# Products as pairs of 64 weight columns, and seven block products for eight in the aggregations of stage three

## Chip, cores and metric

The kernel runs on one core of a Trainium2 chip. The metric is the device time of one launch in microseconds; lower is better. All data are float32. "Graph" below means one of the 32 items of the batch.

## What is computed

A stack of four graph layers over 32 graphs of 512 nodes with 128 features each. Each layer starts with a layer norm and a Relu, and its result is added to its input. The third layer ("stage three") is itself four feature layers with skip connections; it is where most of the change lies.

```python
def _layer(nodes, adj, ws, bs, wd, bd, wn, bn, wu, bu):      # stage three
    src = nodes @ ws + bs
    src_agg = jnp.einsum('bjv,bij->biv', src, _l2norm(adj, 2))
    dst = nodes @ wd + bd
    dst_agg = jnp.einsum('bjv,bji->biv', dst, _l2norm(adj, 1))
    self_rep = nodes @ wn + bn
    upd = jnp.concatenate([src_agg, self_rep, dst_agg], axis=2)
    return jnp.tanh(upd @ wu + bu)
...
    h = jnp.maximum(_layernorm(x, axis=-1), 0.0)
    x = x + _L0_gnn_ref(h, adj, ...)      # one aggregation with the normed adjacency, leaky relu
    h = jnp.maximum(_layernorm(x, axis=-1), 0.0)
    x = x + _L1_gnn_ref(h, adj, ...)      # two aggregations, elu before, tanh after
    h = jnp.maximum(_layernorm(x, axis=-1), 0.0)
    x = x + _L2_gnn_ref(h, adj, ...)      # stage three: four of the layers above
    h = jnp.maximum(_layernorm(x, axis=-1), 0.0)
    x = x + _L3_gnn_ref(h, adj, ...)      # message, aggregation, GRU gates
```

## The kernel before, in words

**Plan.** The kernel first records every operation (`Plan.op`, line 135) with its engine, an assumed duration (`t_mm`, `t_tt` and the like, lines 319 to 335), and the buffers that it reads and writes. `Plan.order` (line 173) then runs a list schedule over all 32 graphs: each engine takes the operation with the earliest due time, `batch * PERIOD` less the length of the work that hangs on it, whose inputs are there and for whose buffers a place is free. The places are a fixed number per kind (line 299): 8 banks of PSUM, and SBUF tiles of 2, 4 and 8 KB per partition (`s2` 36, `s4` 5, `s8` 10). The order that results is the order of the instructions on each engine; work of two to three graphs is interleaved. Where the plan sees TensorE idle for over 0.7 us, `kept_warm` puts in products of the identity (`ps_idle`, line 1170).

**Data.** An adjacency `a` and its transpose `aT` are 128 partitions by 4 chunks by 512 columns, 8 KB each, loaded anew for each graph on SP's queue. Node features lie either in rows (128 nodes of a chunk on the partitions) or turned (features on the partitions, 512 nodes in the columns). Turning is done by a VectorE transpose of 32x32 blocks and a bounce through DRAM (`turned`, line 705), or, in the first two and the last graph, on TensorE against the identity.

**Products.** `mm` (line 352) records one TensorE product: 128 weight columns, and 128 to 512 columns of data, into one PSUM bank. An aggregation is four such products of 512 columns, one per chunk of 128 nodes. Products of 256 and 128 columns are recorded by `product` in `gates` (515), `seven` (833) and `fifteen` (913).

**Stage three.** After the first two layers, `a` and `aT` are scaled in place, column by column, with the roots of the squared sums (line 1096). The loop at line 1107 then goes through the four feature layers:
- layer 0: `paired_rows` (779) projects the features to source and destination rows `sd`; a node product and eight aggregation products of 512 columns add up in one bank; ScalarE's tanh reads that bank (1136).
- layer 1: `fifteen` (869) turns the features, aggregates them with `aT` and `a` (eight products of 512 columns, `ps_agg<-aT,f1r` and `ps_agg<-a,f1r`, copied out by ScalarE at 894), and then makes layer 1's result and its shares in layers 2 and 3 with fifteen products of 256 columns.
- layer 2: as layer 0, and VectorE adds the share from `fifteen` (1135) before the tanh.
- layer 3: the projections of two feature blocks are made by `seven` (796), a scheme of seven products for eight on halves of nodes and of inputs, with some fourteen VectorE operations; then aggregation as in layer 2.

**GpSimd** takes the power -1/2 for the norms (688) and for the scaling (1077), little else. In the norms, a VectorE operation (`nb`, 696) waits for it.

Of the kernel before, what the change touches and what calls it, by code (L numbers as in the profile page):

```python
# [24 lines left out]
PERIOD = 37.0  # L25
ENDING = -3.5
# [5 lines left out]
GATES = 5 * D  # L32
FIFTEEN = GATES + 4 * D
T_COLS = FIFTEEN + 6 * D
# [247 lines left out]
def gnn_stack(  # L282
# [16 lines left out]
    plan = Plan(sb, psum, {"bank": 8, "s2": 36, "s4": 5, "s8": 10}, {"bank": 0, "s2": 4, "s4": 0, "s8": 0})  # L299
# [12 lines left out]
    def wt(col, n=D):  # L312
        return w_sb[:, col:col + n]
# [37 lines left out]

    def mm(ps, out_of, lhs, rhs, n, start, stop, reads, later=0.0):
        op("PE", t_mm(n), lambda: nc.tensor.matmul(out_of(ps.ap()), lhs(), rhs(), start=start, stop=stop),  # L353
           reads, [ps], later=later)

    LAST = [W_L2[3][0] + (2 * k + o) * D for k in (2, 0) for o in range(2)]
# [11 lines left out]
    def setup():  # L368
# [67 lines left out]
        for at, (b11, b12, b21, b22), wbuf in ((0, LAST, (W2F, {3})), (GATES, BOTH, W3)):  # L436
# [11 lines left out]
        m, c = rf_sb, ROW_OF[3] * 2 * D  # L448
        op("DVE", t_tt(D), lambda: nc.vector.tensor_sub(t_sb[:, 4 * D:5 * D], m[:, c:c + D], m[:, c + D:c + 2 * D]), [RF], [(TS, {4})])
# [33 lines left out]
    def program(b):  # L483
# [13 lines left out]
        def gates(h3T, mT):  # L497
# [17 lines left out]
            def product(o, data, weight, wbuf, first):  # L515
                op("PE", t_mm(H), lambda: nc.tensor.matmul(o[0](), weight(), data[0](), start=first, stop=True, skip_group_check=True), [data[1], wbuf], [o[1]])  # L516

# [209 lines left out]
        def added_rows(x, m, quiet=False):  # L727

            o = buf("s2", rows_shape, "xr")
            if at_ends:  # L730
                ps = plan.bank("t")
                for c in range(NC):
                    op("PE", 0.109, lambda c=c: nc.tensor.transpose(ps.ap()[:, c * P:(c + 1) * P], m.ap()[:, c * P:(c + 1) * P], ident),
                       [m, ID], [(ps, {c})])
# [14 lines left out]
        def transposed(h, name):  # L749
            if at_ends:  # L750
                ps, hT = plan.bank("t"), buf("s2", name=name)
                for c in range(NC):
                    op("PE", 0.109, lambda c=c: nc.tensor.transpose(ps.ap()[:, c * P:(c + 1) * P], h.ap()[:, c, :], ident),
                       [(h, {c}), ID], [(ps, {c})])
                op("ACT", t_act(N), lambda: nc.scalar.copy(hT.ap(), ps.ap()), [ps], [hT])
                return hT
# [22 lines left out]
        def paired_rows(nodes, wcols, wbuf, bias, bbuf, col):  # L779

            sd = buf("s4", (P, NC, 2 * D), "sd")
            for h in range(NC // 2):
                ps = plan.bank("sd")
                for j in range(2):
                    c = 2 * h + j
                    for k, nk in enumerate(nodes):
                        mm(ps, lambda t, j=j: t[:, j * 2 * D:(j + 1) * 2 * D],
                           lambda nk=nk, c=c: nk.ap()[:, c * P:(c + 1) * P],
                           lambda k=k: wt(wcols + k * 2 * D, 2 * D), 2 * D, k == 0, k == len(nodes) - 1, [nk, wbuf])
# [6 lines left out]
        def seven(x1, x2, dst, part, behind):  # L796
# [3 lines left out]
            at = 0  # L800
            (b11, b12, b21, b22), wbuf, (bias, bc), bbuf = LAST, (W2F, {3}), (rf_sb, ROW_OF[3] * 2 * D), RF
            H = N // 2
            s13, s24, ev, dv, xx = (buf("s2", (P, 2, H), k) for k in ("s13", "s24", "ev", "dv", "xx"))
            bank_a, bank_b, bank_c, bank_d = (plan.bank("seven") for _ in range(4))

            def half(m, k):
                return m.ap()[:, k * H:(k + 1) * H]

            def t(k):
                return t_sb[:, at + k * D:at + (k + 1) * D]  # L810

            def dve(o, a, b, reads, writes, sub=False, behind=()):
                op("DVE", t_tt(H), lambda: nc.vector.tensor_tensor(o(), a(), b(), op=ALU.subtract if sub else ALU.add), reads, writes, behind=behind)

            def place(k, o):
                return lambda: dst(k, o)

            def of(m, k):
                return lambda: m.ap()[:, k, :]

            def flat2(m, k):
                return lambda: m.ap()[:, k, :].rearrange("p (j v) -> p j v", j=2)

            def region(ps, k):
                return lambda: ps.ap()[:, k * H:(k + 1) * H]

            def region2(ps, k):
                return lambda: ps.ap()[:, k * H:(k + 1) * H].rearrange("p (j v) -> p j v", j=2)

            def along2(m, c):  # L830
                return lambda: m[:, None, c:c + D].to_broadcast([P, 2, D])

            def product(ps, k, lhs, rhs, reads, behind=()):
                for j in range(2):
                    op("PE", t_mm(D), lambda j=j: nc.tensor.matmul(  # L835
                        ps.ap()[:, k * H + j * D:k * H + (j + 1) * D], lhs()[:, j * P:(j + 1) * P], rhs(),
                        start=True, stop=True), reads, [ps], behind=behind)

            def pair(m):
                return lambda: m.ap().rearrange("p k (j v) -> p k j v", j=2)  # L840


            dve(of(s13, 1), lambda: half(x1, 0), lambda: half(x1, 1), [x1], [(s13, {1})], True, behind)
            product(bank_a, 0, lambda: half(x1, 0), lambda: wt(b11), [x1, wbuf], behind)
            product(bank_a, 1, of(s13, 1), lambda: t(2), [(s13, {1}), (TS, {at + 2})])
            dve(flat2(ev, 0), region2(bank_a, 0), along2(bias, bc + D), [bank_a, bbuf], [(ev, {0})])
# [22 lines left out]
        def fifteen(f1, shares):  # L869
# [70 lines left out]
            def result(i, o):  # L940
                return half(out_of[o], i)
# [279 lines left out]
```

## Time and profile before

| | |
|---|---|
| time, median of 3 runs | 2272.33 us (2272.28 to 2272.53) |
| the profiled execution | 2275.95 us, of it the span from first to last instruction 2274.2 us |
| TensorE clock granted | 1.000 of full speed |
| idle products | 126 MATMUL records, 17.8 us |
| DMA | 263.03 MB, mean 116 GB/s |

The table of costly groups is read so: line, engine, operation, output and inputs by name, size of the weights, size of the data, count; then busy time in all and the mean duration of one; then the idle time of the engine ahead of them. For TensorE, durations of neighbouring products overlap, so the mean of 593 ns is not what a product costs. Some rows that the change touches:

```profile
L353 PE MATMUL ps_agg<-a,sd 128*128 128x512 f32 x768 | 385.3, 593 | 0.0
L353 PE MATMUL ps_agg<-aT,sd 128*128 128x512 f32 x768 | 380.5, 593 | 0.4 <-DVE sd L791 0.2
L353 PE MATMUL ps_sd<-w_sb,f 128*128 128x256 f32 x512 | 145.6, 380 | 0.9 <-ACT f L1112 0.9
L353 PE MATMUL ps_agg<-aT,f1r 128*128 128x512 f32 x256 | 130.7, 592 | 0.0
L1135 DVE TENSOR_TENSOR c<-ps_agg,c 128x512 f32<-128x512 f32 x64 | 43.7, 683 | 4.1 <-PE ps_agg L353 4.0
L813 DVE TENSOR_TENSOR s<-f,s 128x256 f32<-128x256 f32 x64 | 27.0, 422 | 13.1 <-ACT f L1136 13.1
```

### The profile page before, as it was taken

Reading aid. Unit: us, or ns where it says so; the run is one execution under the profiler, and the core shown is the slowest. Engines: PE = TensorE matmul, PEld = TensorE weight load, DVE = VectorE, ACT = ScalarE, POOL = GpSimd, SP = SyncE. Lnnn points to the kernel's source line nnn. Section 1 sums busy time; section 2 is a strip of 40 time slices with the busy share of each in tenths; the row PEclk is TensorE's granted clock in tenths of the full one; section 3 lists DMA queues with packets and bytes.
Section 4 is the critical chain, followed back from the end, with each engine's and each line's share of the span. In section 5 each row is a group of like instructions: output and inputs, shape, how many; then the busy total and the mean of one; then the engine's idle time right before and its main releaser. Section 6 shows DMA issues by size and latency. Waiting matters only on the chain.

```text
span 2274.2 us, 25755 instructions
## 1 busy us (share of the span) xinstructions
PE 2263.3 (100%) x7608; PEld 1311.8 (58%) x7608; DVE 1607.0 (71%) x4346; ACT 1101.4 (48%) x2563; POOL 216.6 (10%) x203
## 2 busy tenths in 40 slices
PE   9999999999999999999999999999999999999999
PEld 6555565555565555555555655555555556555556
DVE  6756676767777777767777777777677777776655
ACT  7643554544445544455544455445555444552422
POOL 2100100100100100001001001000010010010000
PEclk9999999999999999999999999999999999999999
DMA  8032333444333443334443334443344333333212
GB/s 295 29 105 77 111 99 117 139 128 127 119 105 121 130 130 120 107 117 135 132 123 121 104 120 130 130 120 108 115 136 134 122 117 106 121 99 91 79 42 65
DMA packets 199052, 263.03 MB, mean 116 GB/s; under 512 B 25984, under 2 KB 130688, under 8 KB 198912
## 3 DMA queue, kind: packets, MB, share of 16 engines
q1 hardware_dynamic: 198624, 261.26, 37.6%
q8 instruction: 60, 0.98, 0.2%
q14 instruction: 80, 0.66, 0.1%
q10 hardware_dynamic: 288, 0.13, 0.0%
HBM read 199.18 MB, written 62.13 MB: 115 GB/s over the span
## 4 chain that ended last, share of the span: by engine, by line
PE 95%; DMA 2%; DVE 2%; ACT 0%; issue 0%; SPq 0%; POOL 0%; ACTq 0%; DVEq 0%; POOLq 0%
PE ps_agg L353 61%; PE ps_fifteen L914 9%; PE ps_sd L353 7%; PE ps_seven L835 4%; PE ps_seven L516 4%; PE ps_upd L353 3%; PE ps_gate L353 3%; PE ps_lin L353 1%; PE ps_msg L353 1%; PE ps_node L353 1%; DMA last<-turn_last 0%; DMA turned<-turn_turned 0%; DMA bounce<-invT 0%; DMA r_sb<-in_brow 0%; DMA turn_turned<-blk 0%; DMA rows<-bounce 0%
## 5 line engine op out<-in xcount | busy, mean ns | idle before, releaser
L353 PE MATMUL ps_agg<-a,sd 128*128 128x512 f32 x768 | 385.3, 593 | 0.0
L353 PE MATMUL ps_agg<-aT,sd 128*128 128x512 f32 x768 | 380.5, 593 | 0.4 <-DVE sd L791 0.2
L688 POOL TENSOR_TENSOR sc<-v,neg_half 128x4 f32<-128x4 f32 (+1 forms) x127 | 150.6, 1186 | 1710.5 <-DVE v L649 1603.5
L353 PEld LDWEIGHTS ps_agg<-aT,sd 128*128 128x128 f32 x768 | 136.6, 191 | 86.4 <-issue 77.5
L700 ACT ACTIVATE h<-xr,nb,sc 128x128 f32<-128x128 f32 x384 | 157.9, 482 | 49.1 <-DVE nb L696 49.1
L353 PEld LDWEIGHTS ps_agg<-a,sd 128*128 128x128 f32 x768 | 137.0, 191 | 62.0 <-issue 53.8
L353 PE MATMUL ps_sd<-w_sb,f 128*128 128x256 f32 x512 | 145.6, 380 | 0.9 <-ACT f L1112 0.9
L353 PEld LDWEIGHTS ps_sd<-w_sb,f 128*128 128x128 f32 x512 | 94.4, 190 | 77.6 <-issue 61.7
L1136 ACT ACTIVATE f<-c,cf_sb 128x512 f32<-128x512 f32 x64 | 46.2, 722 | 179.8 <-DVE c L1135 179.8
L353 PE MATMUL ps_agg<-f,w_sb 128*128 128x512 f32 x256 | 130.9, 593 | 0.1
L353 PE MATMUL ps_agg<-aT,f1r 128*128 128x512 f32 x256 | 130.7, 592 | 0.0
L353 PE MATMUL ps_agg<-a,f1r 128*128 128x512 f32 x256 | 130.7, 592 | 0.0
L353 PE MATMUL ps_agg<-aT,h 128*128 128x512 f32 (+2 forms) x260 | 128.7, 583 | 0.6 <-ACT h L673 0.6
L353 PE MATMUL ps_agg<-a,rep 128*128 128x512 f32 x256 | 125.5, 592 | 0.0
L353 PE MATMUL ps_agg<-aT,rep 128*128 128x512 f32 x256 | 121.6, 595 | 2.0 <-DVE rep L1049 1.8
L353 PE MATMUL ps_agg<-aT,msg 128*128 128x512 f32 (+1 forms) x264 | 116.7, 579 | 0.0
L791 DVE TENSOR_TENSOR sd<-ps_sd,rf_sb 128x512 f32<-128x512 f32 x128 | 87.9, 687 | 32.3 <-PE ps_sd L353 31.9
L1096 DVE TENSOR_TENSOR a<-a,rows 128x512 f32<-128x512 f32 x128 | 87.2, 687 | 16.7 <-PE ps_agg L353 16.1
L709 DVE STREAM_TRANSPOSE blk<-h 128x512 f32<-128x512 f32 x87 | 61.4, 706 | 51.4 <-ACT h L700 51.2
L1077 POOL TENSOR_TENSOR inv<-stat,neg_half 128x8 f32<-128x8 f32 x32 | 59.4, 1857 | 308.8 <-DVE stat L1076 287.9
L1096 DVE TENSOR_TENSOR aT<-aT,rows 128x512 f32<-128x512 f32 x128 | 86.4, 684 | 2.0 <-PE ps_agg L353 1.9
L1136 ACT ACTIVATE f<-ps_agg,cf_sb 128x512 f32<-128x512 f32 x32 | 22.0, 687 | 131.8 <-PE ps_agg L353 131.8
(229 smaller groups left out, 4424.6 us busy)
## 6 DMA issues: line engine op xcount, KB each, us to landing
aT<-in_adjt SPq DMA_DIRECT2D x124, 512.0 KB, 3.9
turn_turned<-blk SPq DMA_DIRECT2D x696, 64.0 KB, 1.8
turned<-turn_turned SPq DMA_DIRECT2D x174, 256.0 KB, 2.7
a<-in_adj SPq DMA_DIRECT2D x62, 512.0 KB, 7.5
rows<-bounce SPq DMA_DIRECT2D x32, 512.0 KB, 3.7
shares<-bounce SPq DMA_DIRECT2D x32, 512.0 KB, 4.4
x<-in_x SPq DMA_DIRECT2D x32, 256.0 KB, 2.7
out<-xr SPq DMA_DIRECT2D x31, 256.0 KB, 3.1
```

The lines of the kernel that those rows point to most:

```text
L353: op("PE", t_mm(n), lambda: nc.tensor.matmul(out_of(ps.ap()), lhs(), rhs(), start=start, stop=stop), reads, [ps], later=later)
L516: op("PE", t_mm(H), lambda: nc.tensor.matmul(o[0](), weight(), data[0](), start=first, stop=True, skip_group_check=True), [data[1], wbuf], ...
L688: op("POOL", t_pow(n), lambda: nc.gpsimd.tensor_tensor(inv.ap()[:, :n], v8.ap()[:, :n], neg_half[:, :n], op=ALU.pow), [v8, NH], [(inv, {0})])
L700: op("ACT", t_act(D, 2), lambda c=c: nc.scalar.activation(h.ap()[:, c, :], xin.ap()[:, c, :], AF.Relu, bias=nb.ap()[:, c:c + 1], scale=inv ...
L709: op("DVE", t_tt(N), lambda: nc.vector.transpose(blk.ap().rearrange("p b (c r) -> p c b r", c=NC), m.ap().rearrange("p c (b s) -> p c b s" ...
L791: op("DVE", t_tt(N), lambda ps=ps, h=h: nc.vector.tensor_add(sd.ap()[:, 2 * h:2 * h + 2, :], ps.ap().rearrange("p (j v) -> p j v", j=2), a ...
L835: op("PE", t_mm(D), lambda j=j: nc.tensor.matmul(ps.ap()[:, k * H + j * D:k * H + (j + 1) * D], lhs()[:, j * P:(j + 1) * P], rhs(), start= ...
L914: op("PE", t_mm(H), lambda: nc.tensor.matmul(o[0](), weight(), data[0](), start=first, stop=True, skip_group_check=True), [data[1], wbuf], ...
L1077: roots = op("POOL", t_pow(2 * NC) + 0.4, lambda: nc.gpsimd.tensor_tensor(inv.ap()[:, :2 * NC], stat.ap(), neg_half, op=ALU.pow), [stat, N ...
L1096: op("DVE", t_tt(N), lambda m=m, c=c, s=s: nc.vector.tensor_mul(m.ap()[:, c, :], m.ap()[:, c, :], rows.ap()[:, s, :]), [(m, {c}), rows], [ ...
L1136: end = op("ACT", t_act(N, 1), lambda to=to, i=i, f_new=f_new: nc.scalar.activation(f_new.ap(), to.ap(), AF.Tanh, bias=cf_sb[:, i:i + 1]), ...
```

## The change

**Every product in two halves.** `by_halves` issues a product as two, with weight columns 0 to 63 into PSUM partitions 0 to 63 and weight columns 64 to 127 into partitions 64 to 127, over the same data. All of `mm`, the gates' and `fifteen`'s products, the turns on TensorE and the idle products go through it. Each half is issued as a 128x64 tile of the array, at column 0 or 64.

**Seven products for eight in stage three.** The aggregations of the four feature layers are taken as products of 2x2 blocks: two halves of the 128 features, two chunks of nodes, two halves of the 512 columns. The blocks of `a` and `aT` get three combinations each, `made_of`, four GpSimd subtractions of 512 columns per matrix (one in place). The features get four combinations, `left_sums`, on VectorE. `side_by_side` issues two unlike 64-column products as a pair, one on each half of the array; `features` (layers 0, 2 and 3) and `edges` (layer 1) list them and add their results, mostly with VectorE operations of 64 partitions by 256 columns, some on GpSimd. `nodes` products join the same banks by three 256-column products. `seven` is gone: layer 3's projections are plain products of `paired_rows` over two feature blocks.

**Plan.** `PERIOD` 37 to 41, `ENDING` -3.5 to -5.5; places `s2` 26, `s4` 6, a new kind `s6` 5 for the combinations, `s8` 8.

```diff
-PERIOD = 37.0
-ENDING = -3.5
+PERIOD = 41.0
+ENDING = -5.5
...
+HALVES = slice(0, P // 2), slice(P // 2, P)
...
-    plan = Plan(sb, psum, {"bank": 8, "s2": 36, "s4": 5, "s8": 10}, {"bank": 0, "s2": 4, "s4": 0, "s8": 0})
+    plan = Plan(sb, psum, {"bank": 8, "s2": 26, "s4": 6, "s6": 5, "s8": 8}, {"bank": 0, "s2": 3, "s4": 0, "s6": 0, "s8": 0})
...
+    def by_halves(to, weight, data, start, stop):
+        for c in HALVES:
+            nc.tensor.matmul(to[c], weight[:, c], data, start=start, stop=stop, skip_group_check=True)
+
     def mm(ps, out_of, lhs, rhs, n, start, stop, reads, later=0.0):
-        op("PE", t_mm(n), lambda: nc.tensor.matmul(out_of(ps.ap()), lhs(), rhs(), start=start, stop=stop),
-           reads, [ps], later=later)
+        op("PE", t_mm(n), lambda: by_halves(out_of(ps.ap()), lhs(), rhs(), start, stop), reads, [ps], later=later)
...
+        H, Q = N // 2, D // 2
...
+        def made_of(m):
+            tm, even, odd = buf("s6", (P, 2, 3, H), "made"), {0, 2}, {1, 3}
...
+            for o, x, y, reads, writes in (
+                    (t(1), two(m, 1, 1), two(m, 0, 1), [m], [(tm, {1})]),
+                    (two(m, 0, 1), two(m, 0, 1), two(m, 0, 0), [(m, even)], [(m, even)]),
+                    (t(0), two(m, 1, 1), two(m, 0, 1), [m], [(tm, {0})]),
+                    (t(2), two(m, 1, 0), t(0), [(m, odd), (tm, {0})], [(tm, {2})])):
+                summed("POOL", nc.gpsimd, t_pool(N), o, x, y, -1, reads, writes)
+            return tm
...
+        def left_sums(n, part, src, st, place):
+            for k, x, y, sign, reads in (
+                    (0, part(1, 0), part(1, 1), 1, []), (1, place(0), part(0, 0), -1, [0]),
+                    (2, part(0, 0), part(1, 0), -1, []), (3, part(0, 1), place(1), -1, [1])):
+                summed("DVE", nc.vector, t_tt(n), place(k), x, y, sign, [src] + [(st, {j}) for j in reads], [(st, {k})])
+
+        def side_by_side(lo, hi, begun):
+            for pair in zip(lo, hi, strict=True):
...
+                def emit(emits=emits):
+                    for to, lhs, rhs, start in emits:
+                        nc.tensor.matmul(to(), lhs(), rhs(), start=start, stop=True, skip_group_check=True)
+
+                op("PE", t_mm(H), emit, reads, writes)
+
+        def features(i, sd, nodes, made, f_new, more):
...
+            lo = products(A, 1, q4) + products(C, 5, q4) + node(C, 1, 1) + products(A, 2, q4) + node(A, 0, 0) + products(C, 3, q2)
+            hi = products(Bh, 6, q4) + node(Dh, 2, 1) + products(Dh, 3, (2, 3)) + products(Bh, 7, q4)
+            second = len(hi)
+            hi += products(Bh, 4, q4) + node(Bh, 1, 0)
...
+            side_by_side(lo[:4], hi[:4], begun)
+            copy(p1_lo, A)
+            add(d, p1_lo, Bh)
+            if more:
+                copy(p1_hi, A)
+                summed("POOL", nc.gpsimd, t_pool(H), quarter[0, 1][0], quarter[0, 1][0], d[0], 1, [quarter[0, 1][1], d[1]], [quarter[0, 1][1]])
+                d = quarter[0, 1]
+                op("POOL", t_pool(N), lambda: nc.gpsimd.tensor_tensor(
...
+            side_by_side(lo[4:second], hi[4:second], begun)
+            e = quarter[1, 1] if more else (region(p1, 1, 1), (p1, {3}))
+            add(e, e if more else p1_lo, Bh)
+            add(quarter[1, 1], e, C)
+            side_by_side(lo[second:], hi[second:], begun)
+            add(d, d, C)
+            add(quarter[0, 1], d, Dh)
+            if more:
+                add(quarter[0, 0], quarter[0, 0], A)
+            add(quarter[1, 0], quarter[1, 0] if more else p1_lo, Bh)
...
+        def edges(f1r, made, ge):
...
+            left_sums(P, part, f1r, st, lambda k: lambda: st.ap()[:, k])
+            banks = [plan.bank(n) for n in ("a2", "b2", "c2")]
...
-        def seven(x1, x2, dst, part, behind):
...
-            for k, m in enumerate((aT, a)):
-                ps = plan.bank("agg")
-                for c in range(NC):
-                    mm(ps, lambda t: t, lambda c=c: chunk(c), lambda c=c, m=m: m.ap()[:, c, :], N, c == 0, c == NC - 1, [f1r, (m, {c})])
-                op("ACT", t_act(N), lambda ps=ps, k=k: nc.scalar.copy(ge.ap()[:, k, :], ps.ap()), [ps], [(ge, {k})])
+            edges(f1r, made, ge)
...
+        made = [made_of(m) for m in (aT, a)]
         for i, (wsd, wn) in enumerate(W_L2):
...
+            nodes = [(f, wn, (0, None, 1, 2)[i])]
             if i == 3:
-                sd = buf("s4", (P, NC, 2 * D), "sd")
-                seven(f0, f, *of_halves(sd), [third_started])
+                sd = paired_rows([f0, f], [wsd + 4 * D, wsd], (W2F, {i}), rf_sb, RF, ROW_OF[i] * 2 * D)
+                nodes.append((f0, wn + 2 * D, 3))
...
+            end = features(i, sd, nodes, made, f_new, later[i - 2] if i > 1 else None)
...
-            nc.tensor.matmul(ps[:, :P], ident, ident, start=True, stop=True)
+            by_halves(ps[:, :P], ident, ident, True, True)
```

## The prediction

> **What bounds the kernel now.** I read the page's engine line first, then the chain that ended last, then who waited for whom on TensorE, then timelines for the price of one product.
>
> ```profile
> span 2274.2 us, 25755 instructions
> PE 2263.3 (100%) x7608; PEld 1311.8 (58%) x7608; DVE 1607.0 (71%) x4346; ACT 1101.4 (48%) x2563; POOL 216.6 (10%) x203
> ...
> PE 95%; DMA 2%; DVE 2%; ACT 0%; issue 0%; SPq 0%; POOL 0%; ACTq 0%; DVEq 0%; POOLq 0%
> ```
>
> TensorE is busy for all but 11 us of the span, and 95% of the last chain is its own. The list of waits, kept to TensorE, has eight entries, 8 us together; the longest is
>
> ```profile
> PE ps_agg L353 <- DVE rep L1049: 1.8, 3, 1.2
> ```
>
> So the time is the sum of the products' prices. Every f32 product appears as two MATMUL records and two LDWEIGHTS records. The chain in order of time gives the price of 512 columns (24 records are 12 products); the TensorE timeline gives those of 256 and 128, and from the set-up that of one column:
>
> ```profile
> 335.49 10.30 PE ps_agg L353 x24
> ...
> 1000.80 0.59 PE L914 MATMUL ps_fifteen<-xy,w_sb 128*128 128x256 f32 x2
> 1001.24 0.59 PE L914 MATMUL ps_fifteen<-col,t_sb 128*128 128x256 f32 x2
> 1001.67 0.59 PE L516 MATMUL ps_seven<-s,t_sb 128*128 128x256 f32 x2
> 1002.10 1.02 PE L353 MATMUL ps_agg<-f,w_sb 128*128 128x512 f32 x2
> ...
> 1003.61 0.39 PE L835 MATMUL ps_seven<-w_sb,f 128*128 128x128 f32 x2
> 1003.83 0.39 PE L835 MATMUL ps_seven<-t_sb,s 128*128 128x128 f32 x2
> ...
> 21.68 0.73 PE L353 MATMUL ps_foldb<-c_sb,raw 128*128 128x1 f32 x6
> 22.27 0.69 PE L353 MATMUL ps_foldb<-raw,c_sb 128*128 128x128 f32 x4
> ```
>
> Durations overlap, so the price is the distance of starts: 10.30/12 = 0.858 us for 512 columns, (1002.10 - 1000.80)/3 = 0.433 for 256, 0.22 for 128. Per column the slope is (0.858 - 0.433)/256 = 1.66 ns, with some 5 to 8 ns a product on top. At one column, a weight load with its MATMUL takes (22.27 - 21.68)/6 = 98 ns.
>
> For VectorE I need two more readings, of its timeline and of VectorE and GpSimd in the same microseconds:
>
> ```profile
> 1004.11 0.42 DVE L813 TENSOR_TENSOR s<-f,s 128x256 f32<-128x256 f32 x1 [0.34 <-ACT f L1136]
> 1004.45 0.42 DVE L813 TENSOR_TENSOR s<-f,f 128x256 f32<-128x256 f32 x1
> 1004.79 0.42 DVE L813 TENSOR_TENSOR s<-f,s 128x256 f32<-128x256 f32 x1
> ...
> 1040.28 0.69 DVE L1096 TENSOR_TENSOR a<-a,rows 128x512 f32<-128x512 f32 x1
> ...
> 1040.36 1.48 POOL L688 TENSOR_TENSOR sc<-v,neg_half 128x4 f32<-128x4 f32 x1 [10.79 <-DVE v L649]
> ```
>
> A 256-column operation takes 0.42 us, but the next starts after 0.34. And a GpSimd power that takes 1.01 us in its median instance took 1.48 when it started 0.08 us behind a VectorE operation with two SBUF inputs.
>
> **What the Trainium skill says.** "TensorEngine Tiling (Array Packing)", Tiling Modes: in 128x64 mode the array is two tiles that load weights and multiply independently, and a change of mode drains it. "TensorE: Matmul & The Clock Gate", Part 3: multiplications of different tiles start some 4 ns apart, in program order. No run here shows a tiled product yet. "SBUF — State Buffer", Who interferes with whom: a VectorE operation with two SBUF inputs and a GpSimd operation that reads SBUF exclude each other for a whole instruction. The 1.48 us above agrees for the side in which GpSimd comes second; the other side isn't shown. "VectorE: DVE Perf Modes", Two Vector instructions with no wait between them: an operation starting in another group of 32 partitions than its predecessor's operands waits until that one has finished; no run here shows it.
>
> **The change part by part.** I counted the instructions of both programs.
>
> Products, a pair of 64-column halves counted as one. With 512 columns: 1847 before, 695 after. With 256: 1101 and 3405. With 128: 888 and 522, of which 63 and 145 are the idle products that keep TensorE warm. At the old prices that is -1152 x 0.858 = -988, +2304 x 0.433 = +998 and -366 x 0.22 = -81: together -72 us. (The same prices give 2258 for the old program, of 2263 busy.) Behind it: seven-for-eight takes an eighth of the 32 aggregations of 512 columns per graph; the `seven` projections are given back as plain ones; each node product becomes three 256-column pairs; and 82 more idle products cost 18 us.
>
> What a pair costs beyond a whole product is unknown. Each half streams as many columns, so without concurrency the time would double; with it, the second tile's start may add 4 ns at each of two passes, 8 ns x 4622 = 37 us. From below it is 0, as starts of one tile can hide in the other's streaming, and a gain is excluded since the columns stream at one rate. I take the middle, +18.
>
> Issue: a 128-column pair now needs four loads and four MATMULs in 0.22 us. If the 98 ns is issue, it becomes 4 x 98 = 392 ns, +0.17 on 377 non-idle products = +65 us. If it is the loading of 128 columns, 64 take half, 196 ns, and it costs nothing. "TensorE: Matmul & The Clock Gate", LDWEIGHTS, counts by columns, which speaks for the second; I take +10. A 256-column pair has 433/4 = 108 ns for each load and MATMUL, over 98 either way.
>
> VectorE: +896 operations of 256 columns at 0.335 (+300), +123 of 128 at about 0.2 (+25), -64 of 512 at 0.60 (-38), the spacings of full stretches: 1607 + 287 = 1894 us. 832 of the 256-column operations run on 64 partitions; at most they and their successors lose the overlap of 0.085 us, 141 us; I take half, 1964. That is 88% of the time forecast, so it lies beside TensorE; but it runs in order, and its results release products.
>
> GpSimd: 256 operations 128x512, 64 of 64x512, 64 of 64x256. Before shows none of this form. "GPSIMD Engine Reference", 3.1, gives 2.6 cycles per element at 1.2 GHz, thus an estimated 1.11 us and 0.55 us: 390 us, 607 in all, 27%. In a graph the eight `made` operations (9 us) come after the eight row scalings and run beside the transposes by DMA, norm and Relu that lead to `f0`; two turns alone are 2 x (0.7 + 1.8 + 2.7) = 10 us by the page's rows. So they hide; if they were late, the first aggregations would be. The same in-order queue holds the norms' powers: one behind a `made` operation is late by about 1 us, VectorE's `nb` behind it stands, and other VectorE work with it.
>
> ScalarE: 256 more 256-column copies at 0.37, 64 fewer of 512 at 0.58, 64 more tanh pieces: +88 us, 1190, 53%; free. DMA: the same 1382 instructions. Fewer `s8` buffers (8 for 10) leave less run-ahead of loads; at 3.9 to 7.5 us per landing against 71 us per graph, free.
>
> TensorE waited 8 us before; with VectorE at 88% I add +10; the bound above is the rival below.
>
> Sum against the profiled execution, 2275.95 us (span 2274.2 and 1.75 around it): 2275.95 - 72 + 18 + 10 + 10 = 2242. The median of the runs is 3.6 below the profiled one: 2238.
>
> **Rivals.** First, forecast (60%): TensorE stays the bound, 2200 (no pair cost, no stall) to 2268.
>
> Second (22%), slower: VectorE becomes the bound through the shared port. The place is the 384 GpSimd additions. From 1964 to the 2227 or so that TensorE needs there are 263 us, 0.69 us for each addition; if a running addition holds VectorE's two-input operations longer than that, about two thirds of it, VectorE decides. At 85% of 390 us: 1964 + 332 + 14 at the ends = 2310; at all of it 2368. For: VectorE works nearly without pause and over a third of its operations have two SBUF inputs. Against: it may meet several one-input operations first, and in the trace GpSimd was the one to wait.
>
> Third (10%): the halves run side by side only in part, because a weight load can't go ahead of the multiplication in front of it. With 98 ns exposed at two starts per pair: 2238 + 4622 x 0.196 = 3140; with no concurrency at all 4400. For: nothing before shows tiles. Against: loads hide completely now, also at 128 columns.
>
> Fourth (5%): costs and gain cancel, within 0.2% of 2272, about what a measurement can tell from no change. The last 3% lies below 2200.
>
> **How the numbers follow.** Faster 0.62, same 0.05, slower 0.33 (the second, the third and a cent of spill). Predicted 2238. The range takes the forecast's own 2200 to 2268, the neutral case and the second up to 2325, leaving out its upper end, the third and the last.
>
> **What would show it.** Right: starts of 256-column pairs about 0.44 us apart, the two halves' records overlapping, TensorE near 100%, VectorE near 88% and its two-input rows near 0.42. Wrong by the second: VectorE at 95% and more, two-input rows clearly longer, TensorE waits on `ps_ab` or `ps_cd` for VectorE. Wrong by the third: pairs 0.6 us or more apart with nobody waiting. Wrong in small: 128-column pairs at 0.39.

## The result and the profile after

| | before | after |
|---|---|---|
| time, median | 2272.43 us (2272.28 to 2273.19) | 2401.44 us (2398.68 to 2405.63) |
| ratio | | 1.0569, 95% interval 1.055 to 1.0587 |
| span of the profiled execution | 2274.2 us | 2399.1 us |

The changed kernel is 129 us slower. These are the page's engine line and its shares of the chain that ended last (the last work of the kernel, followed back to what released it), of the kernel after:

```profile
span 2399.1 us, 49973 instructions
PE 2271.5 (95%) x18520; PEld 1402.5 (58%) x18520; DVE 2078.2 (87%) x5305; ACT 1186.3 (49%) x2819; POOL 741.6 (31%) x587
...
PE 33%; DVE 19%; POOL 8%; DMA 2%; ACT 2%; issue 1%; SPq 0%; DVEq 0%; POOLq 0%; ACTq 0%
```

TensorE now stands still for 2399.1 - 2271.5 = 128 us of the span, where it was 11 before, and it carries a third of the last chain where it carried 95%. The shares listed cover 65% of the span; of it VectorE has 19% and GpSimd 8%, where they had 2% and nothing, though neither is full: 87% and 31% busy. The waits of TensorE in the kernel after (engine and tile, what it waited for, us in total, times, longest):

```profile
PE ps_fifteen L356 <- DVE ge L812: 52.8, 26, 2.9
PE ps_ab L858 <- DVE c L812: 27.9, 31, 1.0
```

Twenty-six and thirty-one times, in 32 graphs: each is something that happens once per graph. None of TensorE's waits is on a combination by GpSimd (`made`). TensorE's timeline around the first wait, in one graph (start, duration, group, count of records, and the idle time ahead with its releaser):

```profile
1035.93 0.59 PE L356 MATMUL ps_agg<-aT,h 128*64 128x512 f32 x1
...
1036.35 1.88 PE L356 MATMUL ps_agg<-aT,h 128*64 128x512 f32 x7
1040.17 0.65 PE L356 MATMUL ps_fifteen<-ge,w_sb 128*64 128x256 f32 x4 [1.94 <-DVE ge L812]
1040.95 0.65 PE L356 MATMUL ps_fifteen<-q,t_sb 128*64 128x256 f32 x4
1041.43 0.60 PE L356 MATMUL ps_fifteen<-xy,w_sb 128*64 128x256 f32 x4
1041.86 1.03 PE L356 MATMUL ps_agg<-aT,h 128*64 128x512 f32 x4
1042.72 0.60 PE L356 MATMUL ps_fifteen<-dif,w_sb 128*64 128x256 f32 x4
```

A product of two halves now has four records, and when TensorE is not waiting it costs what a whole one did: 1041.86 - 1041.43 = 0.43 us for 256 columns, 1042.72 - 1041.86 = 0.86 for 512. The wait costs more than its 1.94. The record at 1035.93 and the seven at 1036.35 are two products of 512 columns; at 0.858 us each the next product could have started at 1037.65. It started at 1040.17, 2.5 us later. What kept `ge` is seen on VectorE (first fence) and GpSimd (second) in the same microseconds:

```profile
1035.06 0.29 DVE L658 TENSOR_SCALAR v<-mv 128x4 f32<-128x4 f32 x1
1035.27 0.70 DVE L718 STREAM_TRANSPOSE blk<-y 128x512 f32<-128x512 f32 x1
1037.56 1.22 DVE L705 SCALAR_TENSOR_TENSOR nb<-mv,sc 128x4 f32<-128x4 f32 x1 [1.59 <-POOL sc L697]
1038.81 0.85 DVE L812 TENSOR_TENSOR ge<-p,ps_b 64x256 f32<-64x256 f32 x2
```

```profile
1035.28 1.28 POOL L812 TENSOR_TENSOR a<-a 128x512 f32<-128x512 f32 x1
1036.52 1.01 POOL L697 TENSOR_TENSOR sc<-v,neg_half 128x4 f32<-128x4 f32 x1
1037.49 1.26 POOL L812 TENSOR_TENSOR made<-a 128x512 f32<-128x512 f32 x1
```

The norm's `v` is there at 1035.35. Its power `sc` stands in GpSimd's queue behind the combination `a<-a` until 1036.52. VectorE's `nb` waits for `sc` 1.59 us, and `ge`, which needs nothing of the norm, stands behind `nb` in VectorE's order. Then `nb`, four columns wide, takes 1.22 us: it begins 0.07 us after the next combination did and ends 0.03 us after that one's end. `ge` follows, and TensorE stands still until it comes. The Trainium skill, "SBUF — State Buffer", Who interferes with whom, calls the ports that the two engines share an exclusive lock and has the order of issue decide who blocks; here VectorE is second, the side that the kernel before did not show.

How often `nb` was blocked shows in its row (count, then busy and mean ns of one, then idle before). First the kernel before, then the kernel after, with rows of other operations that read two SBUF inputs (`xr`, `a`) and of `stat`, which has one input and eight columns:

```profile
L738 DVE TENSOR_TENSOR xr<-turned,xr 128x512 f32<-128x512 f32 x58 | 40.0, 689 | 27.8 <-DMA turned<-turn_turned 27.6
...
L696 DVE SCALAR_TENSOR_TENSOR nb<-mv,sc 128x4 f32<-128x4 f32 x127 | 20.5, 161 | 41.1 <-POOL sc L688 39.7
...
L1076 DVE TENSOR_SCALAR stat<-stat 128x8 f32<-128x8 f32 x32 | 4.7, 146 | 0.5 <-ACT sq L1072 0.5
```

```profile
L1220 DVE TENSOR_TENSOR a<-a,rows 128x512 f32<-128x512 f32 x128 | 126.8, 998 | 10.8 <-PE ps_agg L356 9.5
...
L746 DVE TENSOR_TENSOR xr<-turned,xr 128x512 f32<-128x512 f32 x58 | 55.5, 958 | 4.5 <-DMA turned<-turn_turned 4.5
...
L705 DVE SCALAR_TENSOR_TENSOR nb<-mv,sc 128x4 f32<-128x4 f32 x127 | 51.4, 405 | 45.3 <-POOL sc L697 45.2
...
L1200 DVE TENSOR_SCALAR stat<-stat 128x8 f32<-128x8 f32 x32 | 32.7, 1021 | 2.6 <-ACT sq L1196 2.6
```

With the scalings `a<-a,rows` (687 ns a piece before) these four rows alone are 40 + 15 + 31 + 28 = 114 us longer. GpSimd pays as well: these are the two costliest of the six rows of its combinations in the kernel after:

```profile
L812 POOL TENSOR_TENSOR made<-aT 128x512 f32<-128x512 f32 x64 | 118.0, 1843 | 207.2 <-DVE aT L1220 170.9 <-issue 27.8 <-DMA a<-in_adj 6.3
...
L812 POOL TENSOR_TENSOR made<-a 128x512 f32<-128x512 f32 x64 | 92.8, 1450 | 5.9 <-DVE inv L1202 2.2 <-DVE a L1220 1.9 <-DVE v L1111 1.2
```

One that is not kept out takes 1.26 to 1.28 us, as in the timeline above.

My theory after this reading: the additions on GpSimd, by keeping VectorE out and by queueing ahead of the powers, cost most of the 129 us. The rivals: the halves themselves cost; VectorE has simply too much work; the places, cut to make room for `made`, have loosened the order.

### The profile page after: what moved, and what is told of

The parts are those of the page before. It is cut to its first block, busy times and chain, and to the rows that moved or that the text cites. A ratio compares the mean times of both kernels' runs of the same rounds, so it can differ in the third digit from the quotient of the medians.

```text
span 2399.1 us, 49973 instructions
## 1 busy us (share of the span) xinstructions
PE 2271.5 (95%) x18520; PEld 1402.5 (58%) x18520; DVE 2078.2 (87%) x5305; ACT 1186.3 (49%) x2819; POOL 741.6 (31%) x587
## 4 chain that ended last, share of the span: by engine, by line
PE 33%; DVE 19%; POOL 8%; DMA 2%; ACT 2%; issue 1%; SPq 0%; DVEq 0%; POOLq 0%; ACTq 0%
PE ps_ab L858 9%; PE ps_sd L356 6%; PE ps_cd L858 5%; POOL made L812 5%; PE ps_agg L356 4%; PE ps_fifteen L356 3%; PE ps_seven L356 3%; DVE c L812 2%; DVE aT L1220 2%; PE ps_gate L356 2%; DVE rep L1173 1%; ACT h L709 1%; DVE bn L655 1%; DVE blk L718 1%; DVE nb L705 1%
## 5 line engine op out<-in xcount | busy, mean ns | idle before, releaser
L858 PE MATMUL ps_ab<-made,st 128*64 128x256 f32 x1536 | 404.7, 381 | 3.1 <-DVE p L812 1.4
L356 PE MATMUL ps_sd<-w_sb,f 128*64 128x256 f32 x2048 | 271.1, 380 | 0.5 <-DVE c L1032 0.2
L858 PE MATMUL ps_ab<-aT,sd 128*64 128x256 f32 x768 | 230.0, 382 | 5.8 <-DVE c L812 3.3
L858 PE MATMUL ps_ab<-a,sd 128*64 128x256 f32 x768 | 228.6, 380 | 0.0
L858 PEld LDWEIGHTS ps_ab<-made,st 128*64 128x64 f32 x1536 | 207.2, 137 | 34.2 <-ACT p L903 10.9
L858 PE MATMUL ps_cd<-aT,st 128*64 128x256 f32 x768 | 211.7, 384 | 1.1 <-DVE c L812 1.0
L858 PE MATMUL ps_cd<-a,st 128*64 128x256 f32 x768 | 211.0, 380 | 0.0
L858 PE MATMUL ps_ab<-made,sd 128*64 128x256 f32 x768 | 196.4, 383 | 1.5 <-ACT f L927 1.5
L356 PE MATMUL ps_agg<-aT,rep 128*64 128x512 f32 x512 | 161.6, 595 | 0.3 <-DVE stat L1200 0.2
L356 PE MATMUL ps_agg<-a,rep 128*64 128x512 f32 x512 | 159.3, 592 | 0.0
```

What stands on the lines that cost most here:

```text
L356: nc.tensor.matmul(to[c], weight[:, c], data, start=start, stop=stop, skip_group_check=True)
L858: nc.tensor.matmul(to(), lhs(), rhs(), start=start, stop=True, skip_group_check=True)
```

## Experiments

Twelve kernels ran, each against the kernel before on the same chip (its median was 2271.68 to 2272.43 us). Runs 2, 3, 5, 8 and 9 leave work out: they show what its presence costs, and compute another result.

**1. The halves alone.** Before, with every product by halves and nothing else.

```diff
+    def by_halves(to, weight, data, start, stop):
+        for c in HALVES:
+            nc.tensor.matmul(to[c], weight[:, c], data, start=start, stop=stop, skip_group_check=True)
...
-        op("PE", t_mm(n), lambda: nc.tensor.matmul(out_of(ps.ap()), lhs(), rhs(), start=start, stop=stop),
-           reads, [ps], later=later)
+        op("PE", t_mm(n), lambda: by_halves(out_of(ps.ap()), lhs(), rhs(), start, stop), reads, [ps], later=later)
```

> The kernel before, with nothing changed but that every TensorE product is issued as two halves of 64 weight columns. From the trace of after, 256-column pairs start 0.43 us apart as whole products did, so the first part of the change should cost nothing: 2272, within 5 us. The prediction's own terms (+18 for the second tile's start, +10 for issue of the 128-column pairs) would put it at about 2300. If half of the loss of 127 us sat in the pairs, it would be 2335 or more.

Measured: 2277.43 us, ratio 1.0022 (1.0014 to 1.003). The page's engine line of this run, and then two groups of 128-column products from its TensorE timeline:

```profile
PE 2264.6 (100%) x15376; PEld 1042.5 (46%) x15376; DVE 1607.1 (71%) x4346; ACT 1102.3 (48%) x2563; POOL 216.9 (10%) x203
```

```profile
1007.44 0.39 PE L355 MATMUL ps_seven<-w_sb,f 128*64 128x128 f32 x4
1007.66 0.39 PE L355 MATMUL ps_seven<-t_sb,s 128*64 128x128 f32 x4
```

Twice the instructions, 5 us: 5.0/3844 pairs = 1.3 ns a pair. The 128-column pairs too stand 0.22 us apart, as whole products did. The halves are not the cause.

**2. Without GpSimd's combinations.** After, in the same order; the products that read `made` read plain blocks.

```diff
-                summed("POOL", nc.gpsimd, t_pool(N), o, x, y, -1, reads, writes)
+                op("POOL", t_pool(N), lambda: None, reads, writes)
...
-                return (lambda: tm.ap()[:, pair, j, :]), (tm, {j})
+                return (lambda: m.ap()[:, 2 * pair, :H]), (tm, {j})
```

> After, with GpSimd's eight combinations of adjacency blocks per graph left out (the products read plain blocks instead, so the result is another), the planned order of every engine unchanged. Theory, the shared port and GpSimd's queue make VectorE late: VectorE's busy time falls from 2078 to about 1920, the wait of ps_fifteen on VectorE's ge (53 us) goes, and the time falls to 2230 to 2290. Rival, VectorE is late by its own added work and the order it stands in: the time stays above 2350.

Measured: 2301.83 us, ratio 1.0131 (1.0117 to 1.0145): 100 us less than after, though above the 2230 to 2290 that the theory gave, with VectorE busy for 1973 us. TensorE's longest wait in this run, and then VectorE's row of `nb`:

```profile
PE ps_ab L858 <- DVE c L812: 28.1, 33, 1.0
```

```profile
L705 DVE SCALAR_TENSOR_TENSOR nb<-mv,sc 128x4 f32<-128x4 f32 x127 | 20.9, 165 | 20.3 <-POOL sc L697 20.0
```

The wait for `ge` is gone (1.5 us left) and `nb` is back at its old duration. The other periodic wait, on `c`, has not moved: it has another cause.

**3. The queue filled, nothing read.** As the second, with a memset of about the same length (1.41 us by its row) in place of each combination: GpSimd is about as occupied as in after (713 us for 742), but these instructions do not read SBUF.

```diff
-                summed("POOL", nc.gpsimd, t_pool(N), o, x, y, -1, reads, writes)
+                op("POOL", t_pool(N), lambda: nc.gpsimd.memset(tm.ap(), 0.0), reads, writes)
```

> As the run without the combinations, but in the place of each stands a GpSimd memset of 1536 columns, about as long (1.3 to 1.4 us), which only writes SBUF. GpSimd's queue is as full as in after, but no read of SBUF excludes VectorE. If the exclusion is what costs, it is within 20 us of the run without combinations; if the norms' powers standing behind the combinations cost most, it stays above 2350; a mixture lies between.

Measured: 2310.44 us, ratio 1.0168 (1.0152 to 1.0184). GpSimd's longest row in this run, VectorE's row of `nb`, and GpSimd's timeline ahead of one norm:

```profile
L830 POOL MEMSET made<- 128x1536 f32 x256 | 356.0, 1411 | 5.7
```

```profile
L705 DVE SCALAR_TENSOR_TENSOR nb<-mv,sc 128x4 f32<-128x4 f32 x127 | 20.9, 165 | 20.2 <-POOL sc L697 20.0
```

```profile
774.61 2.70 POOL L830 MEMSET made<- 128x1536 f32 x2
781.86 1.01 POOL L697 TENSOR_TENSOR sc<-v,neg_half 128x4 f32<-128x4 f32 x1 [4.56 <-DVE v L658]
```

So of the 100 us some 9 come with GpSimd being occupied, and 91 with what a memset does not do: read its inputs, and wait for them. The same section of the page says that a GpSimd instruction that only writes does not contend with a VectorE operation of two SBUF inputs; this run agrees, with `nb` at 165 ns beside 256 memsets. What the run does not test is a power that is late in the queue. A memset waits for no scaled block and is not drawn out, so here it had ended 4.56 us before the power's `v` was there. A power that follows a memset begins 0.08 us after its `v` (median of 60); in after, the 27 that stand directly behind `a<-a` begin 1.16 us after theirs, and `nb` waits 45.2 us in all, for 20.0 here. The 91 us hold this lateness as well as the lock; run 12 shows them apart.

**4. The additions on VectorE instead.** After, with combinations and share additions moved from GpSimd to VectorE and the order planned anew: on GpSimd only the powers are left to exclude anybody, and VectorE has all the work.

```diff
-                summed("POOL", nc.gpsimd, t_pool(N), o, x, y, -1, reads, writes)
+                summed("DVE", nc.vector, t_tt(N), o, x, y, -1, reads, writes)
...
-                summed("POOL", nc.gpsimd, t_pool(H), quarter[0, 1][0], quarter[0, 1][0], d[0], 1, [quarter[0, 1][1], d[1]], [quarter[0, 1][1]])
+                summed("DVE", nc.vector, t_tt(H), quarter[0, 1][0], quarter[0, 1][0], d[0], 1, [quarter[0, 1][1], d[1]], [quarter[0, 1][1]])
...
-                op("POOL", t_pool(N), lambda: nc.gpsimd.tensor_tensor(
+                op("DVE", t_tt(N), lambda: nc.vector.tensor_tensor(
```

> After, with the combinations and the additions of shares moved from GpSimd to VectorE and planned there; nothing is left out. VectorE gets 320 operations of 512 columns and 64 of 256, about 213 us more, and loses the exclusion. Theory of the port: the waits on the port go (some 100 to 160 us), VectorE ends at about 2110 us busy, and the time is 2300 to 2400, little different from after. If the port were of no account, VectorE would need about 2290 and the time would be over 2450.

Measured: 2459.21 us, ratio 1.0823 (1.0808 to 1.0838). VectorE is busy for 2135 us, 87% of the longer span, and TensorE's waits are on many of its results. The busy time is near the 2110 of the theory, but the time is over the 2450 that the expectation gave to the rival, so the run does not tell the two apart. The plan, made anew, itself saw TensorE idle for longer: it put in 241 more idle products than after has, which at 0.22 us are 53 us. As planned here, the additions on VectorE cost more than on GpSimd.

**5. VectorE relieved.** As the second, also without the features' combinations on VectorE (`left_sums`), 512 operations; the products read plain features.

```diff
-                summed("DVE", nc.vector, t_tt(n), place(k), x, y, sign, [src] + [(st, {j}) for j in reads], [(st, {k})])
+                op("DVE", t_tt(n), lambda: None, [src] + [(st, {j}) for j in reads], [(st, {k})])
```

> As the run without GpSimd's combinations, planned order unchanged, but VectorE's combinations of features (left_sums, sixteen operations per graph) are left out too; the products read plain features instead. Theory, what remains without the port (2302 where the products alone make about 2205) is VectorE's own added work, in order: with some 150 us of it gone, the time falls to 2225 to 2270. Rival, the rest comes from fewer SBUF places and the plan's start and end: it stays above 2285.

Measured: 2297.65 us, ratio 1.0108 (1.0091 to 1.0125), only 4 us under the second run, though VectorE fell from 1973 to 1822 us. TensorE still waits 26.7 us for `c`. The theory (2225 to 2270) missed: in that order the amount of VectorE's work is not what TensorE pays for. Nor is a held `nb` costly by itself. In this run 23 of them take 1.0 to 1.1 us beside a share addition, and yet TensorE's wait for `ge` stays at 1.3 us; what stands behind the held operation decides.

**6. The places.** Before, with after's places and its `ENDING`, at `PERIOD` 40.

```diff
-PERIOD = 37.0
-ENDING = -3.5
+PERIOD = 40.0
+ENDING = -5.5
...
-    plan = Plan(sb, psum, {"bank": 8, "s2": 36, "s4": 5, "s8": 10}, {"bank": 0, "s2": 4, "s4": 0, "s8": 0})
+    plan = Plan(sb, psum, {"bank": 8, "s2": 26, "s4": 6, "s8": 8}, {"bank": 0, "s2": 3, "s4": 0, "s8": 0})
```

> The kernel before, with the places of after for the same kinds of buffers (s2 26 for 36, s4 6 for 5, s8 8 for 10, three kept for older graphs) and the due times set for them (40 and -5.5); the space saved stays unused. If run-ahead is free, as the prediction had it, 2272 to 2280. If the smaller number of buffers costs part of the rest, 2285 to 2310, and most of it in the first four and the last two graphs.

Measured: 2306.36 us, ratio 1.0149 (1.0134 to 1.0164): the fewer places, with due times set for them, cost the old kernel some 34 us. Of the 30 us by which its profiled execution is longer, some 18 fall in the middle graphs, where the expectation had most of it at the ends.

**7. An order for longer operations.** After, complete, planned with longer durations for VectorE and GpSimd, so that the plan itself leaves room between them.

```diff
-PERIOD = 41.0
-ENDING = -5.5
+PERIOD = 45.0
+ENDING = 0.0
...
-        return 0.065 + 0.058 * pointers + n / 960
+        return 0.08 + 0.058 * pointers + n / 860
...
-        return 0.15 + n / 450
+        return 0.15 + n / 380
...
-            summed("DVE", nc.vector, t_tt(n), o, x, y, 1, reads, writes)
+            summed("DVE", nc.vector, t_tt(n) + 0.09, o, x, y, 1, reads, writes)
```

> After, computing all of it, planned with longer assumed durations: 0.09 us more for the additions on 64 partitions, 1.5 for 1.29 us for GpSimd's combinations, some 12% more for other VectorE operations; due times set again (45 and 0). If after is slow because its order was made with too short durations, this is 2300 to 2350. If the port and VectorE's work limit it in any order, it stays within 30 us of after's 2401.

Measured: 2486.1 us, ratio 1.0941 (1.0925 to 1.0957), worse than after by 85. A miss: the plan put in 248 more idle products and came out with other waits for VectorE (`q` 26 us, `xy` 29 us). It does not tell the theories apart, since exclusions have no place in such a plan.

**8. Without the share additions too.** As the second, also without the 128 additions of shares on GpSimd.

```diff
-                summed("POOL", nc.gpsimd, t_pool(H), quarter[0, 1][0], quarter[0, 1][0], d[0], 1, [quarter[0, 1][1], d[1]], [quarter[0, 1][1]])
+                op("POOL", t_pool(H), lambda: None, [quarter[0, 1][1], d[1]], [quarter[0, 1][1]])
...
-                op("POOL", t_pool(N), lambda: nc.gpsimd.tensor_tensor(
...
+                op("POOL", t_pool(N), lambda: None, [p1_hi[1], (to, {2, 3})], [(to, {2, 3})])
```

> As the run without GpSimd's combinations, planned order unchanged, and GpSimd's additions of shares (four per graph) are left out too, so that GpSimd does the powers alone. Theory of the port: the 128 additions of shares still excluded VectorE for up to 139 us of GpSimd time; without them 2280 to 2295, 5 to 20 below the 2302. If they cost nothing, 2302.

Measured: 2285.02 us, ratio 1.0059 (1.0044 to 1.0074), 17 us less than the second. GpSimd is back at 222 us. `stat`, still at 1.02 us in the second run, is at 0.16 here, in the same order: it was a share addition that held it up.

**9. The eighth with the old number of 2 KB places.**

```diff
-    plan = Plan(sb, psum, {"bank": 8, "s2": 26, "s4": 6, "s6": 5, "s8": 8}, {"bank": 0, "s2": 3, "s4": 0, "s6": 0, "s8": 0})
+    plan = Plan(sb, psum, {"bank": 8, "s2": 36, "s4": 6, "s6": 5, "s8": 8}, {"bank": 0, "s2": 4, "s4": 0, "s6": 0, "s8": 0})
```

> The 2285 us run without GpSimd's combinations and share additions, with 36 places of s2 (4 kept back) for 26 (3), which fits because its 12 KB combinations are never allocated. Theory: part of the 80 us that remain there comes from the smaller number of 2 KB places, so the order gets tighter: 2255 to 2275 us. Rival: what remains is the periodic 0.98 us wait for the second bank and the longer start and end, which the places do not touch: 2280 to 2290.

Measured: 2267.65 us, ratio 0.998 (0.9972 to 0.9987), 17 us less than the eighth. Two of TensorE's waits in this run, and then the row of `stat`:

```profile
PE ps_ab L858 <- ACT p L903: 8.6, 25, 0.6
...
PE ps_ab L858 <- DVE c L812: 1.4, 3, 0.6
```

```profile
L1198 DVE TENSOR_SCALAR stat<-stat 128x8 f32<-128x8 f32 x32 | 5.4, 170 | 7.8 <-ACT sq L1194 7.1
```

The periodic wait for `c`, 28 us in after and in the second run, belonged to the order that the fewer places force. Of the 17 us some 11 are idle products that this order does without (376 records for 580, 51 pairs of 0.22 us). `stat` stays short, at 0.17 us.

**10 and 11. Which places.** Before, `ENDING` -5.5, with only `s8` cut (10), and with only `s2` cut and `s4` 6 (11).

```diff
-    plan = Plan(sb, psum, {"bank": 8, "s2": 36, "s4": 5, "s8": 10}, {"bank": 0, "s2": 4, "s4": 0, "s8": 0})
+    plan = Plan(sb, psum, {"bank": 8, "s2": 36, "s4": 5, "s8": 8}, {"bank": 0, "s2": 4, "s4": 0, "s8": 0})
```

> Before with 8 places of s8 for 10, nothing else but ENDING -5.5. It leaves no work out. Prediction's 'fewer s8 buffers: free' says 2270 to 2276. Rival: the 8 KB places carry the 34 us that the run of before with all of after's places lost, 2295 or more.

```diff
-    plan = Plan(sb, psum, {"bank": 8, "s2": 36, "s4": 5, "s8": 10}, {"bank": 0, "s2": 4, "s4": 0, "s8": 0})
+    plan = Plan(sb, psum, {"bank": 8, "s2": 26, "s4": 6, "s8": 10}, {"bank": 0, "s2": 3, "s4": 0, "s8": 0})
```

> Before with 26 places of s2 (3 kept back) for 36 (4), s4 6 for 5, s8 10 as before, ENDING -5.5. It leaves no work out. Theory: the 2 KB places carry the 34 us lost with all of after's places: 2295 to 2315. Rival: the 8 KB places do, and this one stays at 2270 to 2280.

Measured: 2270.73 us, ratio 0.9995 (0.9986 to 1.0003), and 2317.57 us, ratio 1.0207 (1.0191 to 1.0222). The 8 KB places are free; the 2 KB places cost 45 us. How that looks on TensorE, idle products in the kernel before and in the eleventh run:

```profile
L1170 PE MATMUL ps_idle<-ident 128*128 128x128 f32 x126 | 17.8, 303 | 2.0 <-POOL ident masks.py:199 1.4 <-DVE sd L791 0.6
```

```profile
L1170 PE MATMUL ps_idle<-ident 128*128 128x128 f32 x300 | 41.3, 288 | 1.4 <-POOL ident masks.py:199 1.4
```

TensorE is busy for 99% of that span too: part of the loss (174 records, 87 products of 0.22 us, 19 us) is filled with products of the identity, and no wait shows it.

**12. The complete kernel with more places.** After with 31 `s2` and 4 `s6`.

```diff
-    plan = Plan(sb, psum, {"bank": 8, "s2": 26, "s4": 6, "s6": 5, "s8": 8}, {"bank": 0, "s2": 3, "s4": 0, "s6": 0, "s8": 0})
+    plan = Plan(sb, psum, {"bank": 8, "s2": 31, "s4": 6, "s6": 4, "s8": 8}, {"bank": 0, "s2": 3, "s4": 0, "s6": 0, "s8": 0})
```

> The complete kernel after with 31 places of s2 for 26 and 4 of s6 for 5[...]. It leaves no work out. Theory: places cost some 10 to 30 us of the 129, the exclusion by GpSimd the rest: 2375 to 2395 us. Rival, places cost nothing beside the late norms, or a fourth s6 place missing gives the gain back: within 6 of 2401.

Measured: 2401.59 us, ratio 1.0574 (1.0558 to 1.059), the time of after. TensorE's waits:

```profile
PE ps_fifteen L356 <- DVE ge L812: 51.5, 27, 2.0
PE ps_c L858 <- DVE ge L812: 16.5, 26, 0.7
PE ps_ab L858 <- ACT p L903: 8.6, 26, 0.3
```

The wait for `c` has gone here too (1.9 us), but a second one for `ge` (16.5) and the one for `p` that run 9 has as well have come in its place. The expectation (2375 to 2395) missed: while VectorE is held up once per graph, these places buy nothing, or the `s6` place given up for them costs what they gain; the run does not tell which.

Its trace settles another question, whether the wait for `ge` comes from the power's lateness in GpSimd's queue or from the lock. GpSimd and then VectorE in one graph:

```profile
816.05 1.27 POOL L812 TENSOR_TENSOR a<-a 128x512 f32<-128x512 f32 x1
817.43 1.01 POOL L697 TENSOR_TENSOR sc<-v,neg_half 128x4 f32<-128x4 f32 x1
```

```profile
816.27 1.07 DVE L658 TENSOR_SCALAR v<-mv 128x4 f32<-128x4 f32 x1
818.47 1.23 DVE L705 SCALAR_TENSOR_TENSOR nb<-mv,sc 128x4 f32<-128x4 f32 x1 [0.51 <-POOL sc L697]
```

Here the power begins 0.09 us after its `v`, so it is not late in the queue; instead `v` itself, four columns wide and with one input, is held by `a<-a` and takes 1.07 us where its mean was 0.17 in run 2. It is held so in 27 graphs, `nb` behind it as before, and TensorE's wait for `ge` is the same. The lock alone is enough for it; in after the lateness in the queue takes the part that the lock on `v` has here.

No version that does all the work was faster than the kernel before beyond the noise.

## Why the prediction was wrong

The runs, laid in a row, give the way from what the prediction held to what was measured:

| | us | step |
|---|---|---|
| before, less the products saved (-72, computed) plus the halves (+5, run 1) | 2205 | |
| all of the scheme but GpSimd's additions, 36 places (run 9) | 2268 | +63 |
| 26 places (run 8) | 2285 | +17 |
| share additions on GpSimd (run 2) | 2302 | +17 |
| combinations: GpSimd occupied by them (run 3) | 2310 | +9 |
| combinations: that they read, and wait for what they read (after) | 2401 | +91 |

- **Products, -72: not refuted, not measured alone.** The counts and the prices of a 256- and a 512-column product held (0.43 and 0.86 us). No run isolates the saving. Two small slips of the prediction: its three terms add up to -71, and its eight waits of TensorE to 6 us where it says 8.
- **A pair's second tile, +18, and issue, +10: right in kind, too large.** Together 5 us. TensorE's timeline of after shows why the first is small: the two tiles start 0 to 0.01 us apart, and both halves of a pair fit into the old spacing:

```profile
1002.42 0.38 PE L858 MATMUL ps_cd<-a,st 128*64 128x256 f32 x1
1002.42 0.38 PE L858 MATMUL ps_ab<-made,st 128*64 128x256 f32 x1
1002.63 0.38 PE L858 MATMUL ps_cd<-a,st 128*64 128x256 f32 x1
1002.64 0.38 PE L858 MATMUL ps_ab<-made,st 128*64 128x256 f32 x1
```

- **The third rival, halves only partly side by side, is out** by the same lines and by run 1. The fourth is out by the time.
- **VectorE, 1894 by count and 70 for held operations: close.** Without any addition on GpSimd it was busy for 1927 and 1936 us (runs 8 and 9), which leaves 33 to 42 for the holding where it took 70, if the count is right. What the sum lacked is the exclusion: 2078 in after, +151 over run 8. The share of 88% was forecast and 87% came, over a longer span, so the number looked right while its parts were not.
- **The step that failed: "with VectorE at 88% I add +10; the bound above is the rival below".** TensorE stands still 128 us. The prediction treated VectorE as harmless until it was full, and the second rival began only where VectorE's busy time passes TensorE's (263 us of exclusion, 0.69 us an addition). Exclusion added about 151 us, well below that, and still cost about 108 (91 for the combinations, 17 for the share additions, each with its lateness in the queue). In-order work is late long before the engine is full: one `nb` held up 1.6 us for its input and 1.1 us by the lock puts `ge` and TensorE back by 2.5 us, once per graph; 26 times that is an estimated 65 us.
- **The norms: seen, and not priced.** The prediction wrote that a power behind a combination would be "late by about 1 us", that `nb` "stands, and other VectorE work with it". That is what happened, to the microsecond (`sc` from 1035.35 to 1036.52). It gave this no term, and it did not see that `nb` has two SBUF inputs and meets the next combination at once. Run 3 has no such lateness, so its 9 us are not the price of it; run 12 shows that the wait for `ge` comes without it too, by the lock alone.
- **`made` hidden: right.** TensorE never waits for a combination. Their work is hidden; what they do to their neighbours is not. Their price was low too: 607 us of GpSimd forecast, 742 measured.
- **"Fewer `s8` buffers ... free": right (run 10); the places that mattered were not mentioned.** The diff cuts `s2` from 36 to 26 as well. That costs the old kernel 45 us (run 11) and this one, without GpSimd's additions, 17; in the complete kernel a part of them given back is worth nothing (run 12), so the 17 is not simply a share of the 129.
- **The second rival, 2310 to 2368: the shared port was right, its measure was not.** It called for VectorE at 95% and more. The longer two-input rows came, with VectorE at 87%; its highest time was 33 us short of the measured one. The waits on `ps_ab` came too, but they are no sign of it: they stay in run 2 without the combinations, and go with more places (run 9). The wait that the lock made is on `ps_fifteen`.

Open is the first step of the table, 63 us, or 74 if one counts that run 9 has 51 idle pairs fewer than the -72 includes. About 17 of it lie at the ends: the first product of `ps_fifteen<-q` starts at 80.1 us in run 9 and 75.4 before, and from that of the last graph to the end it takes 77.1 us for 64.7. In between, from one graph's first such product to the next one's, it takes 69.5 us before, 68.7 in run 9, 69.3 in run 2 and 72.1 in after (means of 20 graphs). For the rest the trace of run 9 has some 130 short waits of TensorE, mostly for VectorE and ScalarE, 29 us together, and each may cost more than it shows, as the wait for `ge` above did (2.5 us for 1.94). Run 5 speaks against the amount of VectorE's work as their cause, in the order with 26 places; no run splits this further, nor was the -72 tried by itself. The granted clock was 0.989 to 0.994 in the four runs of after, and 0.999 to 1.000 in runs 2 and 3. If it slowed every product in proportion, 0.005 to 0.011 of 2187 us of products at their prices, 11 to 24 us of the 91, would be its part; why it was lower is open.

## What to carry to other kernels

Price an operation that is moved to GpSimd not by its own time but by what it does to VectorE: list VectorE's operations that fall beside it and have two SBUF inputs, or are a `tensor_scalar`, small ones first, and follow what stands behind each in VectorE's order to the engine that sets the time. A busy share below 100% is no slack here: the engine works in order, and its results release the bound engine once per stage. And when a change cuts buffers, run the old kernel with the new numbers first: part of the loss is filled with idle work that no list of waits shows.

## What the runs showed of the hardware

- A four-column VectorE operation (0.16 us) took 1.22 us beside a GpSimd subtraction, and an eight-column one with a single input (`stat`) rose from 0.15 to 1.02 us in after and in runs 2 and 3, where 26 of its 32 instances overlap a share addition; without share additions it was 0.16 and 0.17 (runs 8 and 9), and in run 5, where the work ahead of it is less, 0.21. The section of "SBUF — State Buffer" named above counts `tensor_scalar` among the operations that can take both ports; here the delay showed at eight columns, and at four in run 12 (`v`).
- 64-column weight loads have a mean of 137 ns where 128-column ones had 191 (mean of the loads for `ps_agg<-a,sd`, run 1 and before). The Trainium skill, "TensorE: Matmul & The Clock Gate", LDWEIGHTS, has the load scale with columns; half the columns took 72% of the time here, and twice as many loads still hid (run 1 is 5 us longer in all).
- A pair of 64-column f32 products cost 1.3 ns more than one of 128 columns (run 1), far below the 8 ns that the prediction took as its upper bound.
